# Head logits of a graph-attention layer as full-array bfloat16 products of three parts

## The chip, the cores and the metric

The kernel runs on one core of one Trainium2 chip. Times are device microseconds of one execution; before and after are compared by the median of several. One execution of each kernel was also recorded by the hardware profiler, and its own time stands beside its span below.

## The reference

128 graphs of 128 nodes with 128 features pass four graph layers, each as `x = x + layer(relu(layernorm(x)))`. All four use the same adjacency. What matters here is layer 1, a graph attention with 8 heads of width 32:

```python
h = jnp.einsum('bnf,hfd->bhnd', x, W1)
f1 = jnp.einsum('bhnd,hd->bhn', h, a1[:, :D])
f2 = jnp.einsum('bhnd,hd->bhn', h, a1[:, D:])
e = jax.nn.leaky_relu(f1[..., :, None] + f2[..., None, :], ALPHA)
e = jnp.where(mask[:, None, :, :], e, NEG)
att = jax.nn.softmax(e, axis=-1)
hp = jnp.einsum('bhij,bhjd->bhid', att, h)
```

So the logit of a pair of nodes is a sum of two numbers per head, `f1[h, i] + f2[h, j]`. A second, single-head attention of the same kind follows inside layer 1. Layer 2 is again a single-head attention. Layer 3 takes one of 8 bilinear scores per pair by edge type, then a softmax and two products. Layer 0 mixes pairwise feature differences and is not touched by the change.

## The kernel before, in words

The program has three stages.

1. The pair stage (L312 to L441) works through layer 0's pairwise differences, graph by graph in four blocks, and writes them to HBM.
2. The score stage (L444 to L614) reads them back, forms layer 0's attention and writes its result to HBM.
3. The group stage (L619 to L925) finishes layer 0 and does layers 1 to 3. The change is in this stage, and in a few constants that the setup makes for it (L100 to L102, L133 to L148).

The group stage takes 32 groups of GC = 4 graphs. `group` (L712) is a Python generator, a list of steps parted by `yield`. A loop at the end (L917 to L925) starts a new group every APART = 26 rounds, and in each round takes every running group one step further. So two or three groups are under way at once, in different layers, and their instructions share the queues of the engines. Each engine works its queue in order. The order in a queue is not written out by hand: the framework's scheduler places the instructions when the program is built, starting from the order of the steps, and may interleave steps. A queue's instruction that waits for its operand holds up everything behind it.

The parts of a group that are spoken of below, in the order of the code:

- `po0` (L725 to L730) is the output product of layer 0 and `pad` (L733) the transposed adjacency. `x1` (L736) adds the input.
- `normalised` (L234 to L250) is a layernorm: statistics on VectorE (`ln_s`, `ln_mv`), `ln_ve`, an inverse root as a power on GpSimd (`ln_rs`, L244), and four scalings `ln_xn` on VectorE, one for each graph. It is called three times in a group, for layers 1, 2 and 3.
- `transposed_relu` (L639) transposes the four `ln_xn` on TensorE into `pt` (L642), and ScalarE evicts them as `hTc` (L644). The three calls are the start of layers 1, 2 and 3.
- Layer 1: `pv` (L759) is the projection of all heads, evicted by VectorE as `vals` (L769). `pf` (L764) holds f1 and f2 of the four graphs, those of graph i in partitions 32i to 32i+31. Two ScalarE operations (L774, L776) evict them with a bias that puts ones into the unused rows. `f1d` (L779) spreads f1 over heads as a block-diagonal 128x1024 tile.
- `z` (L787) is the head logits. For each graph two products of 16 rows: 8 rows of f1 against rows of ones, and 8 rows of ones against f2. The 16 rows of graph i lie in the array's rows 32i to 32i+15.
- Prelu and exponential on ScalarE (L794, L795), the mask as a minimum `p` on VectorE (L797), the weighted sums `pa` on TensorE (L801), and `ri` and `xh` on VectorE (L804, L805).
- An elu, the transposes `ptx` (L815), their eviction `xcT` (L818), then the second attention of layer 1: `ph2` (L826), `z2` (L832), the copy `h2` (L834) and `single_head` (L688), which ends with `po` (L676), `ri`, `xh` (L683, L685), an elu (L649 to L652) and `xo` (L709).
- Layer 2 is the same `single_head` behind its own layernorm.
- Layer 3: `pd` (L867), `pv3` (L869, L871), and for each of 8 edge types `pp` (L883), `tt` (L886), `is_t` (L889), `ps` (L893) and `sel` (L896, L898).

Of the kernel before, what the change touches and what calls it, by code (L numbers as in the profile page):

```python
# [24 lines left out]
GC = 4  # L25
NH, DH = 8, 32
# [13 lines left out]
def kernel(ctx: ExitStack, tc: tile.TileContext, x, adj, w, out):  # L40
    nc = tc.nc
# [49 lines left out]
    f1w = cst("f1w", [P, 32])  # L91
    f2w = cst("f2w", [P, 32])
# [4 lines left out]
    aq = cst("aq", [P, NT, P])  # L97
    aqb = cst("aqb", [P, NT])
    vpw = cst("vpw", [P, P])
    head_of = cst("head_of", [P, NH])  # L100
    ones_l = cst("ones_l", [P, 1])
    ones_r = cst("ones_r", [P, 1])  # L102
    shift2 = cst("shift2", [P, 1])
    nc.vector.memset(shift2, -SHIFT)
    bt3 = cst("bt3", [3, P], BF16)
# [5 lines left out]
    with tc.tile_pool(name="wload", bufs=2) as wl, tc.tile_pool(  # L111
        name="wps", bufs=2, space=PSUM
# [16 lines left out]
        transposed(pwT, w["L3_gnn_pw"])  # L129

        nc.vector.memset(f1w, 0.0)  # L133
        nc.vector.memset(f2w, 0.0)
        nc.sync.dma_start(w1c, w["L1_gnn_W1"].rearrange("h f d -> f h d"))
        a1b = wl.tile([P, NH, 2 * DH], F32, tag="a1b", name="a1b")
        nc.sync.dma_start(a1b, bcast(w["L1_gnn_a1"], 0, P))
        for s, dst in ((0, f1w[:, 0:NH]), (1, f2w[:, NH : 2 * NH])):
            prod = wl.tile([P, NH, DH], F32, tag="prod", name="prod")
            nc.vector.tensor_tensor(prod, w1c, a1b[:, :, s * DH : (s + 1) * DH], ALU.mult)  # L140
            nc.vector.tensor_reduce(dst, prod, AX.X, ALU.add)


        of_32 = wl.tile([P, 32], F32, tag="of_32", name="of_32")
        nc.vector.tensor_reduce(of_32, ident.rearrange("p (g k) -> p k g", k=32), AX.X, ALU.add)
        nc.vector.tensor_tensor(head_of, of_32[:, 0:NH], of_32[:, NH : 2 * NH], ALU.add)
        nc.vector.tensor_reduce(ones_l, of_32[:, 0:NH], AX.X, ALU.add)
        nc.vector.tensor_reduce(ones_r, of_32[:, NH : 2 * NH], AX.X, ALU.add)  # L148


        nc.sync.dma_start(w2g[:, :, 0:P], w["L1_gnn_W2"].rearrange("(s k) c -> k s c", k=P))
# [151 lines left out]
    with tc.tile_pool(name="h_pool", bufs=1) as h_pool:  # L303
# [8 lines left out]
        with tc.tile_pool(name="a2", bufs=2) as a2, tc.tile_pool(  # L312
            name="a_d", bufs=3
        ) as a_d, tc.tile_pool(name="a_ph", bufs=3, space=PSUM) as a_ph, tc.tile_pool(
            name="a_ps", bufs=2, space=PSUM
# [82 lines left out]
            for i, (b, q) in enumerate(blocks):  # L398
# [41 lines left out]
                start=True, stop=True,  # L440
# [178 lines left out]
    with tc.tile_pool(name="c1", bufs=1) as c1, tc.tile_pool(name="c2", bufs=2) as c2, tc.tile_pool(  # L619
        name="c3", bufs=3  # L620
    ) as c3, tc.tile_pool(name="c8", bufs=8) as c8, tc.tile_pool(
        name="c_ps", bufs=4, space=PSUM
# [89 lines left out]
        def group(g):  # L712
# [45 lines left out]
            for i in range(GC):  # L758
                nc.tensor.matmul(pv[:, i, :], h1T[:, i, :], w1c, start=True, stop=True)  # L759

            pf = c_ps.tile([P, 2, P], F32, tag="ps", name="pf")
            for s, fw in ((0, f1w), (1, f2w)):
                for i in range(GC):
                    nc.tensor.matmul(  # L764
                        pf[32 * i : 32 * i + 32, s, :], fw, h1T[:, i, :],
                        start=True, stop=True, tile_position=(0, 32 * i),
# [3 lines left out]
                vals.rearrange("p g h d -> p (g h) d")[:, :, 0:DH],  # L770
                pv.rearrange("p g (h d) -> p (g h) d", d=DH),
            )
            f1r = c2.tile([P, P], F32, tag="f1r", name="f1r")
            nc.scalar.activation(f1r, pf[:, 0, :], AF.Identity, bias=ones_r)  # L774
            f2r = c2.tile([P, P], F32, tag="f2r", name="f2r")
            nc.scalar.activation(f2r, pf[:, 1, :], AF.Identity, bias=ones_l)  # L776
            yield
            f1d = c2.tile([P, NH, P], F32, tag="f1d", name="f1d")
            nc.vector.tensor_tensor(f1d, bcast(f1r, 1, NH), bcast(head_of, 2, P), ALU.mult)  # L779
            yield  # L780
            xh = c2.tile([P, GC, NH, DH], F32, tag="xh", name="xh")
            heads = []
            for i in range(GC):
                z = psum2("z")
                rows = slice(32 * i, 32 * i + 16)
                for s in range(2):
                    nc.tensor.matmul(  # L787
                        z[:, s, :], f2r[rows, :], f1d[rows, 4 * s : 4 * s + 4, :],
                        start=True, stop=True, tile_position=(32 * i, 0),
                    )  # L790
# [6 lines left out]
                nc.vector.tensor_tensor(p, p, bcast(mask[:, i, :], 1, NH), ALU.min)  # L797
                yield
                pa = c_ps.tile([P, NH, DH + 1], F32, tag="ps", name="pa")
                for h in range(NH):  # L800
                    nc.tensor.matmul(pa[:, h, :], p[:, h, :], vals[:, i, h, :], start=True, stop=True)  # L801
# [22 lines left out]
            for i in range(GC):  # L824
                for s in range(2):
                    nc.tensor.matmul(  # L826
                        ph2[:, i, 0 : P + 1], xcT[:, s, i, :], w2g[:, s, :],
                        start=s == 0, stop=s == 1,
                    )
            z = psum("z2")  # L830
# [72 lines left out]
            p = short("p3")  # L903
# [61 lines left out]
```

## Time and profile before

| what | value |
|---|---|
| median of 3 executions | 4858.82 us (4854.38 to 4861.73) |
| the profiled execution | 4867.86 us, span 4866.0 us |
| TensorE busy | 3630.9 us, 75% of the span |
| VectorE busy | 3176.1 us, 65% |
| ScalarE busy | 2927.1 us, 60% |
| GpSimd busy | 286.9 us, 6% |
| mean granted TensorE clock | 0.852 of full speed |

In the group stage, from 2850 us of the span to its end, TensorE is busy 1807 of 2016 us, VectorE 1233, ScalarE 818 and GpSimd 164, at a mean clock of 0.83; DMA has a share of 0.08.

How to read the lines that follow. A row of digits is the busy share in 40 equal slices of the span, in tenths. A row of a group of instructions names line, engine, operation, tiles written and read, shape and count, then busy time, mean time of one in ns, and idle time of the engine ahead of it with what ended it. A float32 product shows as two records on TensorE. A record's time is its time in flight; records overlap, so what a product costs is read from one start to the next.

### The profile page before, as it was taken

The numbers are of one execution on the slowest core, as the hardware profiler recorded it, in microseconds if no ns is written. First come the engines' busy times: TensorE is split into PE (matmuls) and PEld (weight loads), VectorE is DVE, ScalarE is ACT, GpSimd is POOL, SyncE is SP. The second block draws the span as 40 slices with busy tenths as digits, with TensorE's granted clock in tenths as the row PEclk, the third lists the DMA queues.
The fourth block names the chain that finished last, engine by engine and source line by source line (L and its number), as shares of the span: only waits on it lengthen the run. The fifth ranks groups of instructions, "written<-read, shape, count | busy, mean of one in ns | idle before, by whom it ended". The sixth has DMA issues, their size and how long they took to land.

```text
span 4866.0 us, 46406 instructions
## 1 busy us (share of the span) xinstructions
PE 3630.9 (75%) x16612; PEld 1818.8 (37%) x16612; DVE 3176.1 (65%) x5517; ACT 2927.1 (60%) x3019; POOL 286.9 (6%) x361
## 2 busy tenths in 40 slices
PE   5666666666666665666666658999999999999997
PEld 1111111111111111222222236666666666666665
DVE  7999999999999984222222235666666566666664
ACT  6888888888888886555555523444444444444443
POOL 0000000000000000000000000000000000000000
PEclk8898999889888887888888867888878797979797
DMA  3333343333333335888888840000000000100000
GB/s 134 158 151 155 150 160 156 153 153 150 154 150 152 157 146 205 319 322 320 311 321 309 316 161 16 22 22 22 22 22 25 20 28 21 29 19 26 18 5 7
DMA packets 219113, 631.21 MB, mean 130 GB/s; under 512 B 36802, under 2 KB 136452, under 8 KB 186116
## 3 DMA queue, kind: packets, MB, share of 16 engines
q1 hardware_dynamic: 218884, 628.25, 34.8%
q8 instruction: 132, 2.16, 0.2%
q14 instruction: 97, 0.79, 0.1%
HBM read 330.93 MB, written 297.25 MB: 129 GB/s over the span
## 4 chain that ended last, share of the span: by engine, by line
PE 46%; DVE 21%; ACT 17%; DMA 10%; issue 4%; POOL 1%; SPq 1%; ACTq 0%; POOLq 0%; DVEq 0%
PE ph L356 9%; ACT d L351 8%; DVE d L348 8%; PE pa L801 6%; DMA v<-v 6%; PE ps L893 5%; PE pp L883 5%; DVE six L377 4%; PE z L787 3%; ACT v L375 3%; PE sc L492 3%; DMA adj<-in_adj 2%; DMA s<-us 2%; PE po L676 2%; ACT v L483 2%
## 5 line engine op out<-in xcount | busy, mean ns | idle before, releaser
L356 PE MATMUL ph<-d,w1T 128*64 128x512 f32 (+1 forms) x4096 | 1154.6, 691 | 620.2 <-ACT d L351 620.1
L348 DVE TENSOR_TENSOR d<-he 128x2048 f32<-128x2048 f32 (+1 forms) x512 | 1150.8, 2249 | 49.6 <-PE ph L356 49.6
L351 ACT ACTIVATE d<-d 128x2048 f32<-128x2048 f32 (+1 forms) x512 | 968.1, 1901 | 31.3 <-DVE d L348 31.0
L356 PEld LDWEIGHTS ph<-d,w1T 128*64 128x64 f32 x4096 | 294.4, 155 | 1446.2 <-ACT d L351 1019.5
L483 ACT ACTIVATE v<-v,h_bi,h_sc 128x2048 f32<-128x2048 f32 (+1 forms) x256 | 528.8, 2077 | 329.0 <-DMA v<-v 322.6
L492 PE MATMUL sc<-v,w_slide 128*32 128x512 f32 (+1 forms) x2048 | 422.4, 710 | 204.7 <-ACT v L483 204.2
L377 DVE BATCH_NORM_STATS2 six<-ph 128x6 f32<-128x512 f32 (+1 forms) x768 | 492.5, 684 | 80.3 <-ACT v L375 80.0
L375 ACT COPY v<-ph 128x1024 f32<-128x1024 f32 (+1 forms) x384 | 387.1, 1008 | 129.6 <-PE ph L356 127.9
L801 PEld LDWEIGHTS pa<-vals,p 128*128 128x128 f32 x2048 | 339.6, 252 | 140.5 <-DVE p L797 105.5
L801 PE MATMUL pa<-vals,p 128*128 128x33 f32 x2048 | 334.4, 320 | 73.3 <-DVE p L797 73.3
L893 PE MATMUL ps<-tt,dstT 128*128 128x128 f32 x2048 | 328.0, 310 | 32.9 <-ACT tt L886 32.9
L893 PEld LDWEIGHTS ps<-tt,dstT 128*128 128x128 f32 x2048 | 286.4, 216 | 94.0 <-ACT tt L886 91.3
L883 PE MATMUL pp<-hTc,aq 128*128 128x512 f32 x512 | 298.4, 667 | 0.0
L244 POOL TENSOR_TENSOR ln_rs<-ln_ve,nhalf 128x4 f32<-128x4 f32 x128 | 160.7, 1256 | 1887.0 <-DVE ln_ve L242 1887.0
L886 ACT ACTIVATE tt<-pp,aqb 128x512 f32<-128x512 f32 x256 | 175.4, 685 | 149.2 <-PE pp L883 148.1
L787 PE MATMUL z<-f1d,f2r 16*128 16x512 f32 x512 | 256.2, 674 | 3.9 <-DVE f1d L779 2.0
L492 PEld LDWEIGHTS sc<-v,w_slide 128*32 128x32 f32 x2048 | 75.2, 119 | 482.3 <-ACT v L483 338.3
L898 DVE COPY_PREDICATED sel<-is_t,ps 128x512 f32<-128x512 int32 x224 | 163.1, 728 | 90.2 <-PE ps L893 85.1
L794 ACT ACTIVATE p<-z 128x1024 f32<-128x1024 f32 x128 | 130.1, 1017 | 122.6 <-PE z L787 122.6
L804 DVE RECIPROCAL ri<-pa 128x8 f32<-128x8 f32 x128 | 26.4, 206 | 251.3 <-PE pa L801 251.3
L379 ACT ACTIVATE v<-ph 128x1008 f32<-128x1008 f32 x128 | 129.2, 1009 | 98.5 <-PE ph L356 98.5
L644 ACT ACTIVATE hTc<-pt 128x512 f32<-128x512 f32 x96 | 57.0, 594 | 206.2 <-PE pt L642 206.2
(224 smaller groups left out, 4437.3 us busy)
## 6 DMA issues: line engine op xcount, KB each, us to landing
v<-v SPq DMA_DIRECT2D x256, 1024.0 KB, 4.9
v<-v SPq DMA_DIRECT2D x256, 1008.0 KB, 6.6
xg<-in_x SPq DMA_DIRECT2D x64, 256.0 KB, 3.2
adj<-in_adj SPq DMA_DIRECT2D x64, 256.0 KB, 4.2
u<-s SPq DMA_DIRECT2D x64, 192.0 KB, 3.9
h<-hT SPq DMA_DIRECT2D x32, 256.0 KB, 2.1
y<-yt SPq DMA_DIRECT2D x32, 256.0 KB, 2.5
yt<-y SPq DMA_DIRECT2D x32, 256.0 KB, 2.8
```

The lines of the kernel that those rows point to most:

```text
L348: nc.vector.tensor_tensor(dv, shifted, bcast(hb[:, i0 : i0 + QR], 2, w_), ALU.subtract)
L351: nc.scalar.activation(d[:, 0 : QR * w_], d[:, 0 : QR * w_], AF.Abs)
L356: nc.tensor.matmul(ph[64 * a : 64 * a + 64, t, 0 : 8 * w_], w1T, d[:, k : k + 8 * w_], start=True, stop=True,)
L375: nc.scalar.copy(vq, ph[:, :, 0:n])
L377: nc.vector.bn_stats(six[:, 2 * q + t, :], ph[:, t, 0:n])
L483: nc.scalar.activation(v[:, 0:n], v[:, 0:n], AF.Prelu, bias=h_bi, scale=h_sc, alpha=0.01)
L492: nc.tensor.matmul(sc[QR * q : QR * q + QR, 0:n], w_slide[:, 30 - 2 * k : 62 - 2 * k], zs[q // 2][:, at : at + n], start=k == 0, stop=k == ...
L787: nc.tensor.matmul(z[:, s, :], f2r[rows, :], f1d[rows, 4 * s : 4 * s + 4, :], start=True, stop=True, tile_position=(32 * i, 0),)
L801: nc.tensor.matmul(pa[:, h, :], p[:, h, :], vals[:, i, h, :], start=True, stop=True)
L883: nc.tensor.matmul(pp, aq[:, t, :], h3T, start=True, stop=True)
L886: nc.scalar.activation(tt, pp, AF.Identity, bias=aqb[:, t : t + 1])
L893: nc.tensor.matmul(ps[:, i, :], dstT[:, i, :], tt[:, i, :], start=True, stop=True)
```

## The change

The logits are no longer made from 16 float32 rows of one graph. The values f1 and f2 are split into three parts that bfloat16 holds exactly (high, middle, low, whose sum is the float32 value), and all 128 rows of the array take part:

- `f1w` and `f2w` hold the 8 head columns three times, so that `pf` has, for each graph, 24 rows: three copies of each head.
- Four VectorE operations turn `pf` (128 x 256: f1 and f2 side by side) into the parts. `fa` is the bfloat16 rounding, `fr` subtracts it in the rows of the second and third copy, `fb` rounds again, `f` subtracts that in the rows of the third copy. `parts_m` holds the factors 0 or -1 of each row. The two ScalarE evictions with bias go away.
- `f1d` becomes bfloat16 and `f2g`, one more VectorE operation, is f2 kept in its graph's own rows alone, for each of the four graphs.
- The logits of a graph are four bfloat16 products over all 128 rows in place of two float32 products over 16: `own_rows` (ones in the graph's own rows) against `f1d`, and `f2g` against `head_at` (ones at each head's rows), added up in PSUM.
- The `yield` between the evictions and `f1d` is gone, so a group has one step less.

```diff
-        for s, dst in ((0, f1w[:, 0:NH]), (1, f2w[:, NH : 2 * NH])):
+        for s, dst in ((0, f1w), (1, f2w)):
             prod = wl.tile([P, NH, DH], F32, tag="prod", name="prod")
             nc.vector.tensor_tensor(prod, w1c, a1b[:, :, s * DH : (s + 1) * DH], ALU.mult)
-            nc.vector.tensor_reduce(dst, prod, AX.X, ALU.add)
+            for k in range(3):
+                nc.vector.tensor_reduce(dst[:, k * NH : (k + 1) * NH], prod, AX.X, ALU.add)
...
+        nc.vector.tensor_copy(head_of, parts)
+        nc.vector.tensor_copy(head_at, bcast(parts, 2, P))
...
+        nc.vector.tensor_copy(own_rows, bcast(rows_g, 2, P))
+        nc.vector.tensor_reduce(parts_m[:, 0:1], of_32[:, NH : 3 * NH], AX.X, ALU.add)
+        nc.vector.tensor_reduce(parts_m[:, 1:2], of_32[:, 2 * NH : 3 * NH], AX.X, ALU.add)
+        nc.vector.tensor_scalar(parts_m, parts_m, -1.0, None, ALU.mult)
...
-            f1r = c2.tile([P, P], F32, tag="f1r", name="f1r")
-            nc.scalar.activation(f1r, pf[:, 0, :], AF.Identity, bias=ones_r)
-            f2r = c2.tile([P, P], F32, tag="f2r", name="f2r")
-            nc.scalar.activation(f2r, pf[:, 1, :], AF.Identity, bias=ones_l)
-            yield
-            f1d = c2.tile([P, NH, P], F32, tag="f1d", name="f1d")
-            nc.vector.tensor_tensor(f1d, bcast(f1r, 1, NH), bcast(head_of, 2, P), ALU.mult)
+            fa = c2.tile([P, 2 * P], BF16, tag="fa", name="fa")
+            fr = c2.tile([P, 2 * P], F32, tag="fr", name="fr")
+            fb = c2.tile([P, 2 * P], BF16, tag="fb", name="fb")
+            f = c2.tile([P, 2 * P], BF16, tag="f", name="f")
+            pff = pf.rearrange("p s n -> p (s n)")
+            nc.vector.tensor_copy(fa, pff)
+            nc.vector.scalar_tensor_tensor(fr, fa, parts_m[:, 0:1], pff, ALU.mult, ALU.add)
+            nc.vector.tensor_copy(fb, fr)
+            nc.vector.scalar_tensor_tensor(f, fb, parts_m[:, 1:2], fr, ALU.mult, ALU.add)
+            f1d = c2.tile([P, NH, P], BF16, tag="f1d", name="f1d")
+            nc.vector.tensor_tensor(f1d, bcast(f[:, 0:P], 1, NH), bcast(head_of, 2, P), ALU.mult)
+            f2g = c2.tile([P, GC, P], BF16, tag="f2g", name="f2g")
+            nc.vector.tensor_tensor(f2g, bcast(f[:, P : 2 * P], 1, GC), own_rows, ALU.mult)
             yield
             xh = c2.tile([P, GC, NH, DH], F32, tag="xh", name="xh")
             heads = []
             for i in range(GC):
                 z = psum2("z")
-                rows = slice(32 * i, 32 * i + 16)
                 for s in range(2):
                     nc.tensor.matmul(
-                        z[:, s, :], f2r[rows, :], f1d[rows, 4 * s : 4 * s + 4, :],
-                        start=True, stop=True, tile_position=(32 * i, 0),
+                        z[:, s, :], own_rows[:, i, :], f1d[:, 4 * s : 4 * s + 4, :],
+                        start=True, stop=False,
+                    )
+                for s in range(2):
+                    nc.tensor.matmul(
+                        z[:, s, :], f2g[:, i, :], head_at[:, 4 * s : 4 * s + 4, :],
+                        start=False, stop=True,
                     )
```

More of the change, by code (lines that the diff above doesn't have):

```diff
@@ L99 @@
     vpw = cst("vpw", [P, P])
-    head_of = cst("head_of", [P, NH])
-    ones_l = cst("ones_l", [P, 1])
-    ones_r = cst("ones_r", [P, 1])
+    head_of = cst("head_of", [P, NH], BF16)
+    head_at = cst("head_at", [P, NH, P], BF16)
+    own_rows = cst("own_rows", [P, GC, P], BF16)
+    parts_m = cst("parts_m", [P, 2])
     shift2 = cst("shift2", [P, 1])
@@ L137 @@
         nc.sync.dma_start(a1b, bcast(w["L1_gnn_a1"], 0, P))
-        for s, dst in ((0, f1w[:, 0:NH]), (1, f2w[:, NH : 2 * NH])):
+        for s, dst in ((0, f1w), (1, f2w)):
             prod = wl.tile([P, NH, DH], F32, tag="prod", name="prod")
             nc.vector.tensor_tensor(prod, w1c, a1b[:, :, s * DH : (s + 1) * DH], ALU.mult)
-            nc.vector.tensor_reduce(dst, prod, AX.X, ALU.add)
+            for k in range(3):
+                nc.vector.tensor_reduce(dst[:, k * NH : (k + 1) * NH], prod, AX.X, ALU.add)
         of_32 = wl.tile([P, 32], F32, tag="of_32", name="of_32")
         nc.vector.tensor_reduce(of_32, ident.rearrange("p (g k) -> p k g", k=32), AX.X, ALU.add)
-        nc.vector.tensor_tensor(head_of, of_32[:, 0:NH], of_32[:, NH : 2 * NH], ALU.add)
-        nc.vector.tensor_reduce(ones_l, of_32[:, 0:NH], AX.X, ALU.add)
-        nc.vector.tensor_reduce(ones_r, of_32[:, NH : 2 * NH], AX.X, ALU.add)
+        parts = wl.tile([P, NH], F32, tag="parts", name="parts")
+        nc.vector.tensor_reduce(
+            parts, of_32[:, 0 : 3 * NH].rearrange("p (k h) -> p h k", h=NH), AX.X, ALU.add
+        )
+        nc.vector.tensor_copy(head_of, parts)
+        nc.vector.tensor_copy(head_at, bcast(parts, 2, P))
+        rows_g = wl.tile([P, GC], F32, tag="rows_g", name="rows_g")
+        nc.vector.tensor_reduce(
+            rows_g, ident.rearrange("p (g k) -> p g k", k=32)[:, :, 0 : 3 * NH], AX.X, ALU.add
+        )
+        nc.vector.tensor_copy(own_rows, bcast(rows_g, 2, P))
+        nc.vector.tensor_reduce(parts_m[:, 0:1], of_32[:, NH : 3 * NH], AX.X, ALU.add)
+        nc.vector.tensor_reduce(parts_m[:, 1:2], of_32[:, 2 * NH : 3 * NH], AX.X, ALU.add)
+        nc.vector.tensor_scalar(parts_m, parts_m, -1.0, None, ALU.mult)
         nc.sync.dma_start(w2g[:, :, 0:P], w["L1_gnn_W2"].rearrange("(s k) c -> k s c", k=P))
@@ L784, in group @@
                 z = psum2("z")
-                rows = slice(32 * i, 32 * i + 16)
                 for s in range(2):
                     nc.tensor.matmul(
-                        z[:, s, :], f2r[rows, :], f1d[rows, 4 * s : 4 * s + 4, :],
-                        start=True, stop=True, tile_position=(32 * i, 0),
+                        z[:, s, :], own_rows[:, i, :], f1d[:, 4 * s : 4 * s + 4, :],
+                        start=True, stop=False,
+                    )
+                for s in range(2):
+                    nc.tensor.matmul(
+                        z[:, s, :], f2g[:, i, :], head_at[:, 4 * s : 4 * s + 4, :],
+                        start=False, stop=True,
                     )
```

## The prediction, on record before the changed kernel was run

> **What bounds the kernel now.** I read the page first, to find the stage that the change is in.
>
> ```profile
> PE   5666666666666665666666658999999999999997
> ...
> PEclk8898999889888887888888867888878797979797
> ...
> L787 PE MATMUL z<-f1d,f2r 16*128 16x512 f32 x512 | 256.2, 674 | 3.9 <-DVE f1d L779 2.0
> ```
>
> The last 16 slices are the stage of layers 1 to 3. The lower row is the granted clock. TensorE is over 90% busy there; VectorE has 6 in most of these slices. The 512 records of L787 are the product that is changed; their 256 us are time in flight, not time that could be won. The first and last start of the one `pv` bias product of each group (L869) are 2991.4 and 4832.0 us: 31 spacings of 59.4 us a group. I work out one group's spacing and multiply by 31.
>
> Next I read what TensorE waits for in this stage (the waits from 2900 us on: total us, times, longest).
>
> ```profile
> PE pa L801 <- DVE p L797: 73.3, 32, 2.5
> PE ps L893 <- ACT tt L886: 32.9, 42, 0.8
> ...
> PE pt L642 <- DVE ln_xn L247: 11.8, 4, 4.9
> ```
>
> About 2.3 us a group before `pa`, 0.8 to 1.0 before `ps`, and almost nothing (4 times in 96) before the transposes `pt` of L642, although each stands behind a layernorm. Why not? The timeline of TensorE in one group (start, us in flight) shows it.
>
> ```profile
> 4012.57 0.60 PE L733 MATMUL pad<-ident,adf 128*128 128x128 f32 x4
> 4013.00 1.02 PE L883 MATMUL pp<-hTc,aq 128*128 128x512 f32 x2
> 4013.86 1.95 PE L826 MATMUL ph<-w2g,xcT 128*128 128x129 f32 x16
> 4015.65 1.88 PE L832 MATMUL z<-xcT,g1bc 128*128 128x512 f32 x4
> 4017.37 0.69 PE L642 MATMUL pt<-ident,ln_xn 128*128 128x128 f32 x4
> ...
> 4025.05 1.98 PE L787 MATMUL z<-f1d,f2r 16*128 16x512 f32 x4
> 4026.96 1.12 PE L883 MATMUL pp<-hTc,aq 128*128 128x512 f32 x2
> 4028.01 1.12 PE L787 MATMUL z<-f1d,f2r 16*128 16x512 f32 x2
> 4029.06 1.77 PE L893 MATMUL ps<-tt,dstT 128*128 128x128 f32 x8
> 4030.76 2.07 PE L787 MATMUL z<-f1d,f2r 16*128 16x512 f32 x2
> ```
>
> The layernorm chain behind `po0` takes 4.9 us (4012.7 to 4017.7 in the chain of waits), and matmuls of 4.8 us, mostly other groups', stand between. The second one has 8.7 us of cover (4024.1 to 4032.8), 5.0 of it the `z` products themselves. So TensorE is the bound only because its queue is filled like this.
>
> Last, the granted clock in windows of 3.41 us; the rows are of L787 alone (width, busy TensorE, busy weight loads, clock).
>
> ```profile
> 4026.02:4029.43 3.41, 2.13 (x5) 0.47 (x3) 1.00 0.01 2
> 4029.43:4032.84 3.41, 2.07 (x2) 0.50 (x2) 0.50 0.00 0
> ...
> 4046.50:4049.91 3.41, 2.81 (x8) 1.31 (x8) 1.00 0.02 5
> 4049.91:4053.32 3.41, 0.48 (x1) 0.00 (x0) 0.50 0.00 0
> ```
>
> In this group the clock drops twice, each time after a window mostly filled by the 16-row product. Over the stage the mean clock is 0.83, so a third of it, some 20 us a group, runs at half clock.
>
> [...] The trace has the two values and the width. It also shows drops after windows in which TensorE never idled (3.41 of 3.41 busy), so I take it that 16 rows count for little[...] two float32 records of `pp` take 0.86 us (4013.00 to 4013.86)[...]. [...]
>
> **The change, part by part**, per group of four graphs.
>
> *The products.* Removed: 16 float32 records, which hold TensorE for 1.91 + 1.05 + 2.01 + 3.29 = 8.3 us by the starts in the timeline (the last block from 4047.1 to 4050.4). Added: 16 bfloat16 products of 0.215 = 3.4 us. Gain 4.8 us. If each took the 0.384 us that the bias product of L725 is in flight, 6.1 us, the gain would be 2.1. The separate weight loads hide under the streams.
>
> *VectorE.* Added: copy `fa` and subtraction `fr` on 256 columns from PSUM, 0.42 each (row `xh` L805, 128x256); `fb`, 0.29 (between nothing and the 0.41 of a 512-column scalar operation); `f`, 0.42; `f2g`, 0.42, or 0.69 as a plain 512-column operation. `f1d` stays at 1.21[...]. That is 2.0 us more, beside an engine that is a third idle. Removed from ScalarE: `f1r` and `f2r`, 0.73 us. None of it costs by itself.
>
> *The order.* A group has one step less, so everything from the head logits on comes earlier against its neighbours; and with shorter products the build orders the queues otherwise. I read the built order of the changed kernel and priced it with durations of the trace. Three waits appear before L642's transposes.
>
> A, layer 1's transposes. `ptx`, `ph2`, `z2` now stand ahead of `po0`. Between `po0` and the first transpose only `pad` (0.43) and one `ps` (0.86) are left: 1.3 us of cover. Chain: on VectorE the minimum of layer 1's second head is ahead of `x1`. It waits for `z2`, four Prelu (1.25) and an exponential (0.63), so `x1` starts 0.6 late. Then 4.9 us, plus a `sel` copy of 0.7 that is now queued ahead of `ln_ve`, less 0.8 because one of four `ln_xn` is enough to begin. 5.4 - 1.3 = **4.1 us**.
>
> B, layer 2's. Cover after `po`<-`h`: `ps`, `pp`, `ps` (2.6), two graphs' `z` (1.7) and waits within it of 1.6, so 5.9. Chain on VectorE in its new order, start to start: `ri`, `fr`, `xh` 1.2; `fb`, `sel`, `f`, `is_t` 1.6; `f1d`, `f2g` 1.5; `ex`, `sel`, `ex`, `xo` 2.5; statistics 1.4; the power on GpSimd under a `p` minimum, 1.2; first `ln_xn` 0.3. That is 9.7: the three-part split lies inside layer 2's chain. **3.8 us**.
>
> C, layer 3's. `ri` of the third graph's `pa` is now ahead of the statistics, so these begin only when `pa` is done. From there: 0.2 + statistics and `xh` 1.6 + `sel` 0.7 + `p` minimum 1.2 + 0.1 + `ln_xn` 0.3 = 4.1, less one `ps` of 0.86: **3.3 us**. Before, the chain ran while TensorE waited for `pa`.
>
> *Smaller waits.* `ph2` directly behind `ptx` waits for the 1.01 us copy `xcT`: +1.2. `ps` directly behind its `pp` waits for `tt` (0.69 and hand-offs) twice instead of once: +1.1. `z` waits for the longer way to `f2g`: +0.6. `pd` no longer waits: -0.3. `pa` and `pv` keep theirs. Together +2.6.
>
> *Clock.* Drops after `z` should end; but three waits of 3.3 to 4.1 us leave windows nearly empty, and such a window kept it low before (4049.9 to 4053.3, with 1.13 us of work). I take 20 us a group at half clock again. Bounds: all of it recovered, -10; three further windows of half clock, +5.
>
> *Elsewhere.* Setup gains about ten VectorE operations, under 5 us in all, behind weight loads; taken as 0. No load, store or GpSimd operation is added or passed.
>
> **Sum.** -4.8 + 4.1 + 3.8 + 3.3 + 2.6 = +9.0 us a group, 59.4 to 68.4; times 31 is +279 us. Against the profiled execution (4867.86, span 4866.0) that is 5147. This one lies 9 us above the median of 4858.8, so I state 5140 for the median.
>
> **Rivals.**
> 1. *Faster: the clock is what counts.* If full-row products keep the clock up in every window, the 20 us at half clock return 10 us a group: 9.0 - 10 = -1, 4828 us. It decides as soon as more than 9 of those 20 us are recovered. For it: both drops shown follow `z`. Against: A, B and C each empty a window. Chance 0.06.
> 2. *The waits are half as long* (cover I miss, faster VectorE starts): 9.0 - 5.6 = +3.4, 4964 us. For it: VectorE has slack. Against: the chains are latency, with durations of this trace. 0.18.
> 3. *The waits bring more half clock:* +14, 5293 us. For it: TensorE idles about 18 us of 68. 0.18.
> 4. *The change does less than it says:* the order hardly matters and only the shorter products show behind other waits, within 0.2%. 0.02.
> My forecast has 0.56.
>
> **Numbers.** A difference of 0.2% is about what a measurement can tell from no change. The range runs from just over rival 2 to just under rival 3: 4990 to 5270. Faster 0.06, same 0.02, slower 0.92.
>
> **What would show it.** Right: waits of 3 to 4 us before L642's transposes on `ln_xn` in nearly every group; spacing near 68; TensorE's digits falling from 9 to 7; the new products 0.2 us apart; `fa` to `f2g` near 2 us. Wrong: `pt` still covered, a spacing below 60, or a mean clock above 0.95 (rival 1) or below 0.78 (rival 3).

## The result and the profile after

The changed kernel takes 5239.15 us (median of 4, 5231.13 to 5248.03). The kernel before, run beside it on the same chip, takes 4859.99. The ratio is 1.0783, with a 95% interval of 1.0762 to 1.0804: 379 us slower. The forecast was 5140 us, in a range of 4990 to 5270. The profiled execution took 5248.03 us, with a span of 5246.3 and a mean clock of 0.843 (0.852 before).

The page of the changed kernel first: the slices of TensorE, the slices of the granted clock, and the group of L656, which are layernorm's transposes (L642 before).

```profile
PE   5666666666666656666666677777777777777777
PEclk8889988988988978888888677888888888878888
L656 PE MATMUL pt<-ident,ln_xn 128*128 128x128 f32 x384 | 109.6, 420 | 364.9 <-DVE ln_xn L261 364.9
```

The last 16 slices went from 9 to 7, and the clock stayed at about 8. So TensorE is no longer the bound of the stage; it waits. What it waits for from 2900 us on (total us, times, longest):

```profile
PE pt L656 <- DVE ln_xn L261: 364.9, 96, 4.6
PE pa L826 <- DVE p L822: 59.0, 33, 3.1
PE ps L918 <- ACT tt L911: 56.5, 72, 0.9
PE ph L851 <- ACT xcT L843: 35.3, 32, 1.1
...
PE z L807 <- DVE f1d L798: 13.8, 32, 3.5
```

Before, `pt` waited 4 times, for 11.8 us; now it waits at all 96 places (three in each of 32 groups) for 364.9, or 11.4 us a group. The starts of the `pv` bias product (now L894) go from 2999.6 to 5211.5 us: 31 spacings of 71.35 us, where there were 59.37. The difference of 12.0 us, times 31, is 371 of the 380 us between the two profiled executions.

The middle one of the three waits, in TensorE's timeline (start, us in flight, and in brackets the idle time ahead with its releaser):

```profile
4111.26 1.16 PE L690 MATMUL po<-h,p 128*128 128x130 f32 x8
...
4114.95 1.16 PE L918 MATMUL ps<-tt,dstT 128*128 128x128 f32 x8 [0.78 <-ACT tt L911]
4116.34 0.60 PE L807 MATMUL z<-f1d,own_rows 128*128 128x512 bf16 x2 [0.23 <-DVE f1d L798]
4116.78 0.59 PE L812 MATMUL z<-head_at,f2g 128*128 128x512 bf16 x2
...
4122.86 1.24 PE L656 MATMUL pt<-ident,ln_xn 128*128 128x128 f32 x4 [4.62 <-DVE ln_xn L261]
```

Two of the new products start within 0.44 us (4116.34 to 4116.78), so they run 0.22 us apart (0.216 is the median of the group stage at full clock), as forecast. But after the first two graphs' `z` TensorE starts nothing until layer 2's `ln_xn` comes. This is wait B of the prediction: 4.62 us. In the same stretch A, ahead of layer 1, is 3.45 us and C, ahead of layer 3, is 3.80; over the 32 groups A, B and C average 3.47, 4.49 and 3.44 us.

The waiting instruction holds up what stands behind it: the sums `pa` of the first graph, queued behind these transposes, start at 4123.89, though VectorE had finished their `p` at 4121.55.

The granted clock follows each of these waits. The trace of before holds 414 clock records, that of the changed kernel 454; their values are 1.00 and 0.50, and each but the last lasts a multiple of 3.41 us (3.41 to 44.4 us before). The windows of 3.41 us here and below are cut along these records. Four windows of the changed kernel, two with a wait and the one behind each (width, busy TensorE, weight loads, VectorE, ScalarE, GpSimd, clock, DMA share, GB/s):

```profile
4117.92:4121.33 3.41, 0.32 (x2) 0.00 (x0) 3.31 (x12) 3.32 (x4) 0.83 (x1) 1.00 0.00 0
4121.33:4124.75 3.42, 1.89 (x9) 1.67 (x9) 2.52 (x7) 0.60 (x1) 1.09 (x1) 0.50 0.00 0
...
4145.23:4148.64 3.41, 0.01 (x1) 0.04 (x1) 2.51 (x7) 1.26 (x2) 1.85 (x1) 1.00 0.00 0
4148.64:4152.05 3.41, 3.28 (x8) 1.68 (x8) 1.21 (x4) 0.60 (x1) 0.00 (x0) 0.50 0.00 0
```

A window with 0.32 or 0.01 us of work is followed by one at half clock. So it is throughout: within the 31 spacings all 63 full-clock windows with less than 1 us of work are followed by half clock, and none of the 259 with more than 2.5 us. Over the 31 spacings the half clock takes 24.6 us a group, where it took 18.5.

### The profile page after: what moved, and what is told of

It reads as the page before. It is cut to its first block, busy times and chain, and to the rows that moved or that the text cites. A ratio compares the mean times of both kernels' runs of the same rounds, so it can differ in the third digit from the quotient of the medians.

```text
span 5246.3 us, 46477 instructions
## 1 busy us (share of the span) xinstructions
PE 3616.7 (69%) x16612; PEld 1801.4 (34%) x16612; DVE 3221.4 (61%) x5686; ACT 2904.5 (55%) x2955; POOL 311.7 (6%) x361
## 4 chain that ended last, share of the span: by engine, by line
PE 40%; DVE 22%; ACT 18%; DMA 10%; issue 6%; POOL 3%; SPq 1%; POOLq 0%; ACTq 0%; DVEq 0%
PE ph L370 9%; ACT d L365 8%; DVE d L362 6%; DMA v<-v 6%; PE pa L826 5%; PE pp L908 4%; DVE six L391 4%; PE ps L918 3%; POOL ln_rs L258 3%; ACT v L389 3%; PE sc L506 3%; PE po L690 2%; DMA s<-us 2%; PE pv L773 2%; ACT v L497 2%
## 5 line engine op out<-in xcount | busy, mean ns | idle before, releaser
L506 PE MATMUL sc<-v,w_slide 128*32 128x512 f32 (+1 forms) x2048 | 439.3, 732 | 232.2 <-ACT v L497 217.2
L656 PE MATMUL pt<-ident,ln_xn 128*128 128x128 f32 x384 | 109.6, 420 | 364.9 <-DVE ln_xn L261 364.9
L826 PEld LDWEIGHTS pa<-vals,p 128*128 128x128 f32 x2048 | 307.4, 233 | 118.4 <-DVE p L822 75.4
L826 PE MATMUL pa<-vals,p 128*128 128x33 f32 x2048 | 301.3, 308 | 59.0 <-DVE p L822 59.0
L908 PE MATMUL pp<-hTc,aq 128*128 128x512 f32 x512 | 324.6, 722 | 0.0
L258 POOL TENSOR_TENSOR ln_rs<-ln_ve,nhalf 128x4 f32<-128x4 f32 x128 | 183.9, 1437 | 2073.7 <-DVE ln_ve L256 2073.7
L656 PEld LDWEIGHTS pt<-ident,ln_xn 128*128 128x128 f32 x384 | 68.3, 180 | 428.3 <-issue 238.1
```

The costliest lines, as they stand in the source:

```text
L258: nc.gpsimd.tensor_tensor(rs, ve, nhalf[:, 0:G], ALU.pow)
L506: nc.tensor.matmul(sc[QR * q : QR * q + QR, 0:n], w_slide[:, 30 - 2 * k : 62 - 2 * k], zs[q // 2][:, at : at + n], start=k == 0, stop=k == ...
L656: nc.tensor.transpose(pt[:, g, :], xn[:, g, :], ident)
L908: nc.tensor.matmul(pp, aq[:, t, :], h3T, start=True, stop=True)
```

## The experiments

The expectations speak of three theories. **O**: the order of the queues costs the time. A group has one step less, its later steps stand elsewhere among the other groups' steps, and no other group's matmuls cover the layernorm chains any more. **S**: the split on VectorE costs it, being longer and in layer 2's chain. **R**: a product of 16 rows counts little for the clock.

For each kernel I worked out the same balance from its trace, per group over the 31 spacings: the idle time of TensorE between its instructions, the time at half clock, and the rest. The rest is the spacing less the idle time and less half of the time at half clock: an estimate of TensorE's work as it would be at full clock. It takes work at half clock to last twice as long: two records of L849 (512 columns, float32) start 0.43 us apart at full clock in the trace of before and 0.85 at half clock. The rest is rough, because half-clock windows hold idle time too, and because in e1, e4 to e7 and e11 the trace lacks 63 to 122 of the 512 records of the new products: at 0.22 us each, 0.4 to 0.8 us a group stand there under idle that belong to the rest. "Against before" is the ratio to the kernel before, measured beside it.

| kernel | median us | against before (95%) | spacing us | half clock us | idle us | rest us |
|---|---|---|---|---|---|---|
| before | 4859.99 | 1 | 59.37 | 18.5 | 4.7 | 45.4 |
| changed | 5239.15 | 1.0783 (1.0762 to 1.0804) | 71.35 | 24.6 | 17.1 | 42.0 |
| e1_yield_back | 5029.52 | 1.0379 (1.0320 to 1.0438) | 64.66 | 20.6 | 14.0 | 40.3 |
| e2_before_no_yield | 5158.35 | 1.0647 (1.0627 to 1.0668) | 68.81 | 27.1 | 11.4 | 43.9 |
| e3_before_full_rows | 4818.39 | 0.9935 (0.9913 to 0.9958) | 58.55 | 12.8 | 5.9 | 46.3 |
| e4_after_no_split | 5175.73 | 1.0682 (1.0666 to 1.0698) | 69.92 | 20.4 | 17.5 | 42.2 |
| e5_younger_first | 4952.12 | 1.0202 (1.0184 to 1.0221) | 62.46 | 19.3 | 10.3 | 42.5 |
| e6_apart_25 | 5004.33 | 1.0307 (1.0281 to 1.0333) | 64.15 | 23.2 | 9.8 | 42.7 |
| e7_apart_16_younger | 4540.73 | 0.9354 (0.9334 to 0.9374) | 48.68 | 1.5 | 5.1 | 42.9 |
| e8_before_apart_16 | 4716.69 | 0.9708 (0.9679 to 0.9737) | 54.12 | 10.2 | 1.5 | 47.5 |
| e9_before_full_rows_16 | 4513.43 | 0.9304 (0.9285 to 0.9322) | 48.30 | 0.2 | 2.2 | 46.0 |
| e10_before_16_younger | 4769.04 | 0.9843 (0.9824 to 0.9863) | 55.41 | 12.5 | 1.9 | 47.3 |
| e11_no_split_16 | 4502.90 | 0.9285 (0.9271 to 0.9299) | 47.51 | 0.8 | 4.5 | 42.6 |
| e12_full_rows_own_16 | 4513.92 | 0.9297 (0.9269 to 0.9324) | 47.91 | 0.8 | 1.7 | 45.8 |

The kernel before took 4845.57 us beside e1 to e4, 4857.23 beside e5 to e8, 4849.82 beside e9 to e11 and 4856.68 beside e12. Differences below are each against the before that was measured beside the run.

### e1: the changed kernel with the step boundary put back

```diff
             nc.vector.scalar_tensor_tensor(f, fb, parts_m[:, 1:2], fr, ALU.mult, ALU.add)
+            yield
             f1d = c2.tile([P, NH, P], BF16, tag="f1d", name="f1d")
```

> The changed kernel with the removed step boundary put back ahead of f1d; nothing else differs, all operations are the same. Theory O (the order of the queues opens waits on the three layernorm chains, and these bring half clock): the built order has ptx, ph2 and z2 between other work again, so the wait of layer 1's transposes (3.5 us a group) and the 1.1 us before ph2 shrink, while the waits of layers 2 and 3 stay; spacing of groups 71.4 to some 64 us, 4970 to 5070 us in all. Theory S (the operations added on VectorE cost the time): a step boundary changes nothing, 5239 us within 20.

Measured: 5029.52 us (5001.08 to 5055.63), 184 us over before instead of 379. Not one instruction was removed. The timeline of TensorE shows which wait the boundary takes away:

```profile
4088.74 0.69 PE L656 MATMUL pt<-ident,ln_xn 128*128 128x128 f32 x4
...
4107.19 1.24 PE L656 MATMUL pt<-ident,ln_xn 128*128 128x128 f32 x4 [6.18 <-DVE ln_xn L261]
```

Layer 1's transposes (the first line) no longer wait: `pp` and an older group's `ph2` and `z2` stand between `pad` and `pt` again, 4.4 us of work. The waits of `pt` fall from 96 to 64. C stays (3.70 in the same group), and B grows from 4.62 to 6.18. So the order makes A. The boundary doesn't explain all: with it back, the kernel is still slower, with two of the three waits left. (The interval of its ratio leaves the 184 some 29 us either way.)

### e2: the kernel before without that step boundary

```diff
             nc.scalar.activation(f2r, pf[:, 1, :], AF.Identity, bias=ones_l)
-            yield
             f1d = c2.tile([P, NH, P], F32, tag="f1d", name="f1d")
```

> The kernel before with nothing changed but that the step boundary ahead of f1d is removed: float32 products of 16 rows, no split, no added operation. Theory O: the same kind of waits before the transposes of L642 appear, 8 to 10 us a group against 0.4 before; spacing 59.4 to some 67 us, 5030 to 5150 us. Theory S: no operation is added, so 4860 us within 20.

Measured: 5158.35 us, 313 us slower and 8 us beyond the range of O, with the float32 products of 16 rows and no split at all. Its waits of TensorE from 2900 us on:

```profile
PE pt L642 <- DVE ln_xn L247: 254.9, 95, 4.1
```

One deleted word gives 95 waits of `pt` and 8.0 us of them a group. In one group A is 3.45 us, as in the changed kernel, B 3.62, and C only 1.14. The order alone can make a loss of this size. The 313 and the 379 are not parts of one sum, since e1 shows that the boundary is worth 195 in the changed kernel (379 less 184).

### e3: the kernel before with products over all 128 rows

```diff
-                        z[:, s, :], f2r[rows, :], f1d[rows, 4 * s : 4 * s + 4, :],
-                        start=True, stop=True, tile_position=(32 * i, 0),
+                        z[:, s, :], f2r, f1d[:, 4 * s : 4 * s + 4, :],
+                        start=True, stop=True,
```

> The kernel before, each logit product taking all 128 rows of f2r and f1d in place of the 16 of its graph. Left out: the separation of graphs, so the logits of four graphs are added up. The number, the length and the order of all instructions are those of the kernel before. Theory R (a product of 16 rows counts for little when the clock is decided): time at half clock falls from 18.5 us a group to under 6, spacing 59.4 to 52 to 55 us, 4620 to 4720 us. Rival (only idle time lowers the clock): TensorE is as busy as before, 4860 us within 20.

Measured: 4818.39 us, 0.65% less, with an interval that excludes 1; far from the 4620 to 4720 us of R. First two neighbouring windows of the kernel before, then three of this one, all instructions:

```profile
4026.02:4029.43 3.41, 3.41 (x10) 1.13 (x9) 3.22 (x13) 2.33 (x3) 0.00 (x0) 1.00 0.01 2
4029.43:4032.84 3.41, 3.41 (x11) 1.68 (x10) 3.06 (x7) 0.32 (x1) 1.01 (x1) 0.50 0.00 0
...
4007.98:4011.39 3.41, 3.41 (x10) 1.29 (x8) 2.78 (x6) 2.27 (x4) 0.11 (x1) 1.00 0.02 5
4011.39:4014.81 3.42, 1.35 (x12) 1.21 (x11) 3.30 (x12) 2.87 (x3) 0.36 (x1) 1.00 0.00 0
4014.81:4018.22 3.41, 3.41 (x17) 3.41 (x17) 2.13 (x7) 0.00 (x0) 1.61 (x1) 0.50 0.00 0
```

In the kernel before, TensorE is busy throughout the first window (2.13 us of it `z`), and half clock follows. In this kernel the first of the three windows is full of `z` (8 of its 10 matmuls are L787), and the next one still has clock 1.00. So the drop behind `z` goes, as R says. But the second window has only 1.35 us of work, and the third is at half clock: the drop comes one window later, behind a wait. Half clock fell from 18.5 to 12.8 us (worth 2.9), the idle time rose by 1.2 and the rest by 0.9, which leaves 0.8 of spacing.

### e4: the changed kernel without the split

```diff
-            nc.vector.scalar_tensor_tensor(fr, fa, parts_m[:, 0:1], pff, ALU.mult, ALU.add)
-            nc.vector.tensor_copy(fb, fr)
-            nc.vector.scalar_tensor_tensor(f, fb, parts_m[:, 1:2], fr, ALU.mult, ALU.add)
...
-            nc.vector.tensor_tensor(f1d, bcast(f[:, 0:P], 1, NH), bcast(head_of, 2, P), ALU.mult)
+            nc.vector.tensor_tensor(f1d, bcast(fa[:, 0:P], 1, NH), bcast(head_of, 2, P), ALU.mult)
...
-            nc.vector.tensor_tensor(f2g, bcast(f[:, P : 2 * P], 1, GC), own_rows, ALU.mult)
+            nc.vector.tensor_tensor(f2g, bcast(fa[:, P : 2 * P], 1, GC), own_rows, ALU.mult)
```

> The changed kernel without fr, fb and f: f1d and f2g read the first rounding fa. Left out: the middle and low parts, so the logits are three times the rounded value. VectorE has 1.2 us less a group, all of it in the chain to the logits. Theory O: the order of the products stays and with it the waits; 5239 us within 40. Theory S: the chain to layer 2 is 1.2 us shorter and VectorE freer, 1.2 to 2.4 us a group, 5165 to 5200 us.

Measured: 5175.73 us, 330 us over before, so 49 less than the changed kernel. The size is what S forecast (5165 to 5200 us) and beyond the 40 us that O allowed, but the way is not that of S. S wants a shorter wait B, but it is 4.83 us in the group at 4141, where the changed kernel had 4.62, and all waits of `pt` come to 375.3 us (364.9). VectorE's timeline shows why. First layer 2's chain in the changed kernel:

```profile
4112.56 0.45 DVE L794 SCALAR_TENSOR_TENSOR fr<-fa,parts_m,pf 128x256 f32<-128x256 bf16 x1
...
4116.88 0.72 DVE L923 COPY_PREDICATED sel<-is_t,ps 128x512 f32<-128x512 int32 x1
...
4120.33 1.22 DVE L822 TENSOR_TENSOR p<-p,mask 128x1024 f32<-128x1024 f32 x1
4122.46 1.11 DVE L261 TENSOR_SCALAR ln_xn<-xo,ln_mv,ln_rs 128x128 f32<-128x128 f32 x4 [0.90 <-POOL ln_rs L258]
```

Then the same chain in e4:

```profile
4136.97 1.19 DVE L822 TENSOR_TENSOR p<-p,mask 128x1024 f32<-128x1024 f32 x1
...
4138.17 0.69 DVE L923 COPY_PREDICATED sel<-is_t,ps 128x512 f32<-128x512 int32 x1
...
4138.82 1.22 DVE L822 TENSOR_TENSOR p<-p,mask 128x1024 f32<-128x1024 f32 x1
4140.94 1.12 DVE L261 TENSOR_SCALAR ln_xn<-xo,ln_mv,ln_rs 128x128 f32<-128x128 f32 x4 [0.90 <-POOL ln_rs L258]
```

`fr`, `fb` and `f` are gone (1.2 us), but a minimum of `p` (1.2 us) now stands ahead of `ln_ve` (4138.76), which the power on GpSimd waits for; the second `p` runs beside the power, as in the changed kernel. The `sel` copy only moved: it is the one of 4116.88 in the changed kernel. From the start of `po` to the first `ln_xn` it is 11.2 us in both (4111.26 to 4122.46, 4129.71 to 4140.94). What e4 wins is half clock: 20.4 us a group instead of 24.6, worth 2.1 us, against 1.4 of spacing won. Why there are fewer drops is not shown.

### e5: the changed kernel, younger groups stepped first

```diff
-            running = [gen for gen in running if next(gen, False) is None]
+            running = [gen for gen in running[::-1] if next(gen, False) is None][::-1]
```

> The changed kernel with one line of the stepping loop changed: in each round the younger groups take their step first. Every instruction of the changed kernel is there, in the same number; only their order in the queues differs. Theory O (the order makes the waits): in the built order ptx, ph2 and z2 stand behind the younger group's po0 again, so the wait of layer 1's transposes is covered; the waits before the transposes fall from 11.4 us a group to some 5, spacing 71.4 to 61 to 64 us, 4920 to 5040 us. Theory S (the added operations cost the time): same operations, 5239 us within 30.

Measured: 4952.12 us, 95 us over before. Every instruction of the changed kernel is still there; only the order of the steps within a round differs, and 284 of the 379 us are gone. The waits of TensorE from 2900 us on:

```profile
PE pt L656 <- DVE ln_xn L261: 129.8, 33, 7.6
PE pa L826 <- DVE p L822: 105.3, 32, 3.4
```

So `pt` waits 33 times in place of 96 and 129.8 us in place of 364.9: A and B are nearly gone (0.12 and 0.16 us on average), C stays (3.89). Those of `pa` grow from 59.0 to 105.3 us. Such a move by order alone, larger than all that e4 removed, speaks for O.

### e6: the changed kernel with a new group every 25 rounds

```diff
-APART = 26
+APART = 25
```

> The changed kernel with groups started every 25 rounds in place of 26, which undoes the shift of one step for what comes behind the logits, and shifts what comes ahead of them. Same operations. Theory O: waits before the transposes some 5 us a group, spacing 61 to 64 us, 4920 to 5040 us. Theory S: 5239 us within 30.

Measured: 5004.33 us, 147 us over before. A single round's shift of the groups against each other brings back 232 us; `pt` waits 63 times for 174.5 us, 5.4 a group. e5 and e6 change the order in different ways, and both recover more than half of the loss.

### e7: the changed kernel, younger first, a new group every 16 rounds

```diff
-APART = 26
+APART = 16
...
-            running = [gen for gen in running if next(gen, False) is None]
+            running = [gen for gen in running[::-1] if next(gen, False) is None][::-1]
```

> The changed kernel, younger groups first and groups started every 16 rounds: more groups are under way, so more matmuls are there to fill a wait. Same operations. Theory O: waits before the transposes under 2 us a group and hardly any half clock; spacing 71.4 to 47 to 51 us, 4480 to 4640 us, and not slower than the unchanged kernel in its own order with a start every 16 rounds. Theory S: the added 2.0 us on VectorE become the bound, slower than that one by 2 us a group, 60 us.

Measured: 4540.73 us, 6.5% below before. With more groups under way nearly every chain is covered: from 2900 us on `pt` waits 11 times, for 24.3 us. Half clock is 1.5 us a group, the idle time 5.1.

### e8: the kernel before with a new group every 16 rounds

```diff
-APART = 26
+APART = 16
```

> The kernel before with groups started every 16 rounds in place of 26, nothing else. Theory O: TensorE's waits of 4.7 us a group and much of the half clock go; spacing 59.4 to 48 to 52 us, 4520 to 4680 us. Rival (TensorE's work is the bound at 26 already): 4850 us within 40.

Measured: 4716.69 us, 2.9% below before, and 176 us above e7. The waits went as O says, but the 4520 to 4680 us of O were missed, because the half clock did not go with them: TensorE idles only 1.5 us a group, yet 10.2 us a group run at half clock. The stage of e8 from 3100 to 4400 us:

```profile
3100.00:4400.00 1300.00, 1273.84 (x6855) 870.80 (x6854) 874.95 (x2208) 585.67 (x941) 98.04 (x189) 0.91 0.09 25
```

Busy 1273.84 of 1300 us, and still a clock of 0.91. So idle time alone hardly explains the clock.

### e9: e8 with products over all 128 rows

The edit of e3, on e8. The order of the instructions is the same as in e8 in every queue.

> The kernel before with groups started every 16 rounds, each logit product taking all 128 rows in place of 16; all instructions and their order are those of the unchanged kernel at 16. Left out: the separation of graphs, so the logits of four graphs are added up. There TensorE idles only 1.5 us a group and still has 10.2 us at half clock. Theory R (16 rows count for little when the clock is decided): half clock falls under 3 us a group, worth 3.6, less some 0.8 that the full-row products took more in the earlier full-row run; 4600 to 4660 us. Rival (idle time alone lowers the clock): 4717 us within 25.

Measured: 4513.43 us, 203 us less than e8's median (196 with each against its own before) and more than R forecast. The same stretch:

```profile
3100.00:4400.00 1300.00, 1251.89 (x7649) 907.92 (x7649) 977.02 (x2457) 652.13 (x1060) 106.56 (x209) 1.00 0.09 25
```

TensorE is a little less busy than in e8, and the clock is 1.00. Half clock goes from 10.2 us a group to 0.2, worth 5.0 of the 5.8 us of spacing won. Only the rows of the product changed, and with them its place in the array, so this settles R against its rival: the 16-row product lowers the clock behind it though TensorE is busy, and the product over 128 rows doesn't. Within the 31 spacings 36 of 320 full-clock windows without idle time are followed by half clock in e8, and none of 309 in e9. Whether it is the number of rows or the placing in a part of the array (`tile_position`, which goes too) the runs don't separate. That the logits of e9 are sums over four graphs is not the reason, since e12 has the right ones and the same clock.

### e10: the kernel before with both edits of e7

> The kernel before, younger groups first and a start every 16 rounds: the stepping rule of the fastest run so far, without the change. Theory O with R: the products of the change are worth 3.4 us of work and some 4 of clock a group where the order covers the chains, so this kernel is 150 to 260 us slower than the changed one under the same rule: 4690 to 4800 us. Theory S (the rule does it all and the change is a cost under it too): 4470 to 4540 us.

Measured: 4769.04 us, 81 us below before. e7 differs from it by the whole change and nothing else, and lies 317 below its before. With this stepping the change is thus worth about 236 us, and e7's gain is not that of the stepping alone: e10 has 12.5 us of half clock and a rest of 47.3, e7 1.5 and 42.9. The change that costs 7.8% in one order gains nearly 5% in another. That speaks against S: the added operations go with a gain here, and e2 shows a loss without them. What the change has to give is the clock first (11.0 us less at half clock, worth 5.5), then the shorter products.

### e11: e7 without the split

The edits of e4, on e7.

> The changed kernel, younger groups first, a start every 16 rounds, without fr, fb and f (1.2 us of VectorE a group). Left out: the middle and low parts, so the logits are three times the rounded value. Theory O: TensorE remains the bound and the split is covered; under 0.7 us a group, 4520 to 4545 us. Theory S: VectorE, 78% busy there, sets the pace; 1.2 us a group or more, 4505 us or less.

Measured: 4502.90 us; by the two ratios 34 us less than e7, 1.2 us a group by the spacings (48.68 to 47.51). This is the sum of `fr`, `fb` and `f`, and S had it right here (4505 us or less) where O had not (4520 to 4545). So where the order covers the chains, the split seems to be paid in full. That VectorE sets the pace there is argued, not shown: it is busy for 1015.73 of 1300 us in e7, 78%, against 55% in the changed kernel (709.91).

### e12: the kernel before with full-row float32 products and a new group every 16 rounds

```diff
-APART = 26
+APART = 16
...
+        nc.vector.tensor_copy(own_rows, bcast(rows_g, 2, P))
...
+            f2g = c2.tile([P, GC, P], F32, tag="f2g", name="f2g")
+            nc.vector.tensor_tensor(f2g, bcast(f2r, 1, GC), own_rows, ALU.mult)
...
-                        z[:, s, :], f2r[rows, :], f1d[rows, 4 * s : 4 * s + 4, :],
-                        start=True, stop=True, tile_position=(32 * i, 0),
+                        z[:, s, :], f2g[:, i, :], f1d[:, 4 * s : 4 * s + 4, :],
+                        start=True, stop=True,
```

Here `f2r` is masked to each graph's rows by one VectorE operation per group, so the product over 128 rows holds one graph only.

> A version that the runs point to: the kernel before with a start every 16 rounds, float32 throughout, and f2 kept in each graph's own 16 rows by one more VectorE operation a group (f2g, 0.7 us), so that the logit products take all 128 rows and still compute the reference's logits. No split into parts. Theory O with R: half clock under 1 us a group as in the full-row run, the added 0.7 us covered by a VectorE that is 68% busy; within 25 us of that run, 4480 to 4545 us, about level with the changed kernel under its best rule (4541). Theory S: each added VectorE microsecond is paid, 4535 us or more, slower than the full-row run by 22 us.

Measured: 4513.92 us (4512.02 to 4521.56), 7.0% below before. The mask costs nothing that can be told from e9, and the clock of the stage is full (1.00 from 3100 to 4400 us; 9 in the last 13 slices):

```profile
PEclk8898998889898988788888888789999999999999
```

It is 0.6% below e7 by the ratios (0.9297 against 0.9354, intervals that don't overlap): what the change gave in e7 is had without bfloat16 and without the split. Each of the two was run in one order only (the changed kernel not in that of e8, this one not with younger groups first), so which is quicker at its best is open.

## Why the prediction was right, and where it was off

The direction and the mechanism held: three uncovered layernorm chains in each group, because the order of the queues changed; the step boundary that went is a large part of that, not all (e1). The size was short: +9.0 us a group forecast, +12.0 measured. By its own steps:

- **Products, -4.8: measured -3.4.** Of the 8.3 us of the old products, the two records from 4030.76 to 4032.77 ran at half clock, which is 1.0 too much, and the last block was taken to the end of its flight (3.29 us), where by its starts it holds TensorE for 2.95. Over all groups the starts of L787 lie 0.423 us apart on average at full clock, so 16 are 6.8; the new ones are 3.4. The balance gives the same, 45.4 to 42.0. Most of the missing 1.4 is thus a clock term that the forecast had counted among the products. The 0.215 us of a new product was my estimate, a quarter of the 0.86 us of two `pp` records. That a bfloat16 product takes half a float32 record was not shown: the trace of before holds no bfloat16 product over 128 rows. The runs now show 0.43 us for a float32 record (e9), 0.22 for a bfloat16 one. The weight loads stayed under the products: the new ones start 0.216 us apart although each has a load of 0.098 us (medians).
- **Clock, 0: measured +3.0.** This is the term that was mis-sized most. The prediction took "20 us a group at half clock again". It was 24.6 against 18.5, and half of the 6.1 is 3.0. The drops behind `z` did end: e3 and e9 show that full rows end them. But the three waits bring drops of their own, as the windows above show. The forecast knew this case: its upper bound was +5, from "three further windows of half clock" (10.2 us), and a little over half of that came. In direction this is rival 3, whose 5293 us lie 54 above the result, while the forecast lies 99 below it.
- **Waits A, B, C, 4.1 + 3.8 + 3.3 = 11.2: measured 11.4** a group on average (3.47, 4.49 and 3.44). From this one has to take the 0.4 that `pt` waited before. That the sum fits so well is in part luck: A came out 0.6 smaller and B 0.7 larger.
- **Smaller waits, +2.6: measured about +1.3.** `ph2` 1.10 (1.2 forecast), `z` 0.43 (0.6), `ps` from 1.03 to 1.77 (0.7 instead of 1.1), `pd` down by 0.65. `pa` fell from 2.29 to 1.84, which the forecast kept. All the idle time together rose by 12.4, where the forecast's waits sum to 13.8.
- **The sum.** Idle +12.4, clock +3.0, work -3.4 makes +12.0. Ahead of the 31 spacings, 8 us were lost as well (first `pv` at 2999.6 instead of 2991.4). The forecast took the setup at under 5 us; the same start lies between 2963.9 and 3004.1 in the other kernels, so I read nothing into it.
- **VectorE, 2.0 us: measured 2.04.** `fa` 0.42, `fr` 0.45, `fb` 0.28, `f` 0.47, `f2g` 0.42; `f1d` 1.22 (1.215 before in float32, 1.218 now in bfloat16). `f2g` took the low one of its two prices, 0.42 and not 0.69. No two-input operation in bfloat16 stands in the trace of before, so the 0.42 of `f2g` and the 1.21 of `f1d` were my estimates; why `f2g` is quick for its 512 columns and `f1d` is not for its 1024, the runs do not show. "None of it costs by itself" holds for the changed kernel's waits (e4), though e4 is 1.4 us a group quicker by its clock, and fails where VectorE is 78% busy (e11: 1.2 us a group).
- **"The three-part split lies inside layer 2's chain"** was true and gave 9.7 us for it (10.4 measured, from `po`'s end at 4112.42 to the start of `pt` at 4122.86; the cover of 5.9 us was right, 5.8 measured, so the chain alone makes B too small). But the split doesn't set the chain's length: without it the chain is as long (e4), because a minimum of another group moves into the gap. Of the order, the prediction had A right to the cause: e1 removes it. B and C it put down to the order and the shorter products, and the runs agree only in part. On average over the groups, e2, with the old products, has A 3.48, B 3.44 and C 1.17. In e1, with the old boundary and the new products, they are 0.12, 5.96 and 3.58, and in e5 0.12, 0.16 and 3.89. So A comes with the boundary, C mostly with the new products and what the build makes of them, and B with either, unless the order covers it.
- **Rival 1 (faster, 4828)** failed for the reason that the prediction gave against it. Its mechanism is real all the same: with the chains covered, half clock goes to 1.5 us a group and the changed kernel takes 4541 us (e7). **Rival 2 (waits half as long)** failed: VectorE's slack didn't shorten the chains. **Rival 4 (little effect)** failed too.

One thing is open: why half clock falls by 4 us in e4 with the same waits.

That the rest is 0.9 us a group higher in e3 than before, but 1.5 lower in e9 than in e8, shows in part in the starts of L787 at full clock. Over all rows they lie 0.43 us apart (e3, e9). In the kernel before, 93 of the 353 starts of one 16-row record behind another are less than 0.3 us apart: two graphs' products, in different rows of the array, overlap. In e8 none of 271 is, and 147 of them, next to other products, are more than 0.45 us apart. By these averages full rows cost 0.3 us a group in e3 and save 1.1 in e9.

## What to carry to other kernels

When a change shortens or removes a step in a pipeline of several groups, look first at which other group's work covers the latency chains, and read the built order again: here the same instructions in another order differ by 284 us (e5) and 313 us (e2), while three of the added VectorE operations, taken out, gave 49 (e4) and 34 us (e11). Try the change together with the spacing of the groups before judging it; in the old order it cost 7.8%, with more groups under way it gained 5% over the old kernel in the same stepping. And try a masked product over all rows in place of one that fills few: here a record over all rows took 0.43 us (e3, e9), no more than the small one does on its own, and with the mask the clock held (e12).

## What the runs showed of the hardware

- The clock can fall behind a window without idle time. In e8 TensorE idled 1.5 us of 54.1 a group and ran 10.2 us at half clock; the same order with the product over 128 rows instead of 16 rows ran 0.2 us so (e9), 203 us less in all. How busy TensorE is doesn't decide it alone: in these two runs the rows that are used, or their place in the array, made the difference.
- With full rows, half clock follows windows with little work. In the changed kernel all 63 full-clock windows with under 1 us of work of 3.41 were followed by it, 17 of the 103 with 1 to 2.5 us, and none of the 259 with more. It isn't the work of one window alone: with 1 to 2.5 us, 44 of 62 were in e3, and in e1 27 of the 332 with more than 2.5 us.
- In the changed kernel a wait of about 4 us costs twice: its own time, and then a stretch of half clock. Three waits of 11.4 us a group in all went with 24.6 us at half clock, a loss of 12.3.
- 16-row products in different rows of the array can overlap: in the kernel before 93 of 353 start less than 0.3 us after another, where one alone holds TensorE for 0.43 us.
